# Reordering norm scalings, transposes and a routing product in the last two layers of an eight-sublayer post-norm network

## The chip, the cores and the metric

The kernel runs on one core of a Trainium2 chip. TensorE (PE) multiplies, VectorE (DVE) and ScalarE (ACT) do element work and read PSUM, GpSimd (POOL) does element work on SBUF, SyncE (SP) issues the DMAs. The metric is the device time of one execution in microseconds.

## The reference

Four layers, each an attention-like block and an FFN, and behind each of the eight blocks a residual sum and a layer norm. The input is 2 items of 1024 rows of 1024 channels in float32. The change touches the end of it, layer 2's FFN and layer 3:

```python
x = _layernorm(x + _L2_attn_ref(...))          # selective scan
x = _layernorm(x + _L2_ffn_ref(...))           # int4 weights, x @ w.T + bias
x = _layernorm(x + _L3_attn_ref(...))          # one head of 256, softmax(q k) v Wo + bo
x = _layernorm(x + _L3_ffn_ref(...))
# _L3_ffn_ref
base_out = jnp.einsum('btd,od->bto', x, base_W) + base_b
probs = jax.nn.softmax(logits, axis=-1)        # 15 routes
topk_p, topk_i = jax.lax.top_k(probs, E)       # E = 8
w = jnp.einsum('btk,btke->bte', topk_p, onehot)
h = jnp.einsum('btd,erd->bter', x, A)          # 8 experts of rank 16
lora = jnp.einsum('bter,eor->bto', h * w[..., None], B) * SCALING
return base_out + lora
```

## The kernel before

The two items run one after the other, each through all layers. An item's rows lie in SBUF as `x`, 8 row tiles of 128 rows by 1024 channels, and once more transposed as `xT` (channels on the partitions), which the products read. PSUM is one pool of 8 banks of 128x512 (`ps`, line 70); a new tile takes the bank that has been free longest.

`late` (line 1526) does layer 2's FFN and layer 3 of one item. Its order is written out by hand (`manual_schedule`, line 1745): each engine works off its instructions in program order, and TensorE waits wherever an operand or a bank is not ready. What one row tile `tt` goes through:

- `add_x` (L152): VectorE adds a PSUM tile of a product to half a row tile.
- `stats`: `ln_stats` (bn_stats L163, L164) and `ln_roots`: one small operation of VectorE (L171), Ln and Exp of ScalarE (L177, L178), and four more small ones of VectorE (L180 to L183). L180, L181 and L183 are TENSOR_TENSOR with two inputs in SBUF.
- `ln_scale` (L186): VectorE subtracts the mean and multiplies by the root, in place, one TENSOR_SCALAR over 128x1024.
- `turn_x`: `to_xT` (L124) has TensorE transpose the row tile in 8 pieces (L130) into two PSUM tiles, which VectorE (L97) and ScalarE (L99) copy to `xT`; then GpSimd adds the bias of the next product to the row tile (L1565), in place, once the transposes have read it.

The stages of `late`, in order:

1. `out_proj` (L1567) ends layer 2's attention for rows 512 to 1023 and puts tiles 0 to 3 through norm and `turn_x`. Tiles 4 to 7 get their statistics and roots.
2. int4 FFN, the loop at L1751: step n does the two halves `ffn2(wt, n, 0)` and `ffn2(wt, n, 1)` of row tile n, 8 product calls each (L104). A product call of float32 shows as two matmul records. Behind the first half come `turn_x(n - 1)`, whose norm is of this FFN, and in steps 1 to 3 the scaling and `turn_x` of tiles 4, 5, and 6 with 7, which still lack it.
3. `heads` and `values`: q, k and v.
4. Attention, the loop at L1777: for each query tile `scores` (two PSUM tiles), `exps` (maxima by VectorE, L1635; Exp by ScalarE, L1642), `turn` (8 transposes of the probabilities, L1656, copied by VectorE and ScalarE). From n = 6 on, `join(n - 6)` multiplies the mixed values by Wo, and VectorE adds the result to `x` (L1680), with `stats`. In steps 7 and 8 `turn_x(n - 7)` stands ahead of `join`.
5. `mix(1)`, `turn_x(3)`, `route(0)` (routing logits by `thin`, L112; ScalarE copies them, L1688; transposes L1691; softmax on VectorE), `rank` of four tiles (VectorE), `join` of tiles 4 to 7.
6. `experts(wa, 0)` (L1717): the routes' weights are transposed (L1722) and copied by VectorE to `prT` (L1723); the product with A goes through ScalarE into `hT` (L1726, times 2); a product of `prT` with the one-hot map `oh` spreads the routes over the experts (L1728), and VectorE multiplies `hT` by it (L1729).
7. Base FFN, the loop at L1803: `ffn3(wt, n, 0)` and `ffn3(wt, n, 1)`, 8 calls of the base weights and a ninth of `hT` with B each. `done(n - 1)` scales and stores the tile before. In steps 0 and 1 two tiles each (4, 5 and 6, 7) get `ln_scale` and `turn_x` between the halves. `route(1)`, `rank` and `experts(wa, 1)` for the upper rows are spread over steps 1 to 3.

The weights come by SP into a pool of 8 tiles, each load waiting for the last product that read the tile before; the last two weights of stage 7 are loaded when the last `join` has been done. Rows of biases have a pool of two; a load of a new row waits for the last GpSimd addition of the row it replaces.

Of the kernel before, what the change touches and what calls it, by code (L numbers as in the profile page):

```python
# [12 lines left out]
ALU = mybir.AluOpType  # L13
# [4 lines left out]
P = 128  # L18
# [4 lines left out]
KD = D // P  # L23
# [4 lines left out]
class Net:  # L28
# [1497 lines left out]
    def late(self, b, yd):  # L1526
        nc, i = self.nc, self.i
        NCH, NR = 16, 15
        rows = {"l2_fb": self.row("l2_fb"), "l3_bo": self.row("l3_bo")}
        with self.tc.tile_pool(name=self.nm("l3a"), bufs=1) as lp, self.tc.tile_pool(name=self.nm("l3p"), bufs=2) as tp:  # L1530
# [14 lines left out]
            oh = lp.tile([NR, P], F, name=self.nm("oh"))  # L1545
# [8 lines left out]
            prT = lp.tile([NR, S], F, name=self.nm("prT"))  # L1554
            hT = lp.tile([P, S], F, name=self.nm("hT"))
            wb = self.param(lp, "l3_B", [P, D])
# [5 lines left out]
            def turn_x(tt, row):  # L1562

                self.to_xT(tt)
                nc.gpsimd.tensor_tensor(self.x[:, tt, :], self.x[:, tt, :], row, ALU.add)  # L1565

            def out_proj():  # L1567

                for nh in range(2):
                    acc = [self.ps() for _ in range(4)]  # L1570
                    for c2 in range(NCH // 2):
                        w = self.w(i["l2_out"][nh, c2])
                        y = self.w()
                        for cc in range(2):
                            nc.sync.dma_start(y[:, cc * HALF : (cc + 1) * HALF], yd[2 * c2 + cc][:])
                        for cc in range(2):
                            c = 2 * c2 + cc
                            for tt in range(4):
                                nc.tensor.matmul(  # L1579
                                    acc[tt],  # L1580
                                    y[:, cc * HALF + tt * P : cc * HALF + (tt + 1) * P],
                                    w[:, cc * HALF : (cc + 1) * HALF],
                                    start=c == 0,
                                    stop=c == NCH - 1,
                                )
                        if nh == 0 and c2 == 0:
                            for tt in range(4):
                                self.ln_stats(tt)
                            self.ln_roots(list(range(4)))
                        if nh == 0 and c2 % 2 == 1:  # L1590
                            self.ln_scale(c2 // 2)
                            turn_x(c2 // 2, rows["l2_fb"])
                    for tt in range(4):
                        self.add_x(4 + tt, nh, acc[tt])

            def ffn2(wt, tt, nh):
                p = self.ps()
                self.mm(p, [(self.xcols(k, tt * P, P), wt[k][:, nh * HALF : (nh + 1) * HALF]) for k in range(KD)])
                self.add_x(tt, nh, p)
# [49 lines left out]
            def turn(tt):  # L1649
                th, q = tt // 4, tt % 4  # L1650
                pr, sm = prs.pop(tt)
                for g in range(2):
                    p = self.ps()
                    for j in range(4):
                        kt = 4 * g + j
                        nc.tensor.transpose(p[:, j * P : (j + 1) * P], pr[:, kt * P : (kt + 1) * P], self.ident)  # L1656
                    self.evac(
                        pts[th][:, 4 * g : 4 * g + 4, q * P : (q + 1) * P], p.rearrange("p (k t) -> p k t", k=4)
                    )
                r = rinv[th][:, q : q + 1]  # L1660
                nc.vector.tensor_tensor(r, sm[:, 0:1], sm[:, 1:2], ALU.add)
                nc.vector.reciprocal(r, r)
# [54 lines left out]
            def experts(wa, th):  # L1717

                ts = slice(th * HALF, (th + 1) * HALF)
                p = self.ps()  # L1720
                for j in range(4):
                    nc.tensor.transpose(p[:NR, j * P : (j + 1) * P], st[th][:, j, :], self.ident)  # L1722
                nc.vector.tensor_copy(prT[:, ts], p[:NR, :])  # L1723
                p = self.ps()
                self.mm(p, [(wa[:, k * P : (k + 1) * P], self.xcols(k, th * HALF, HALF)) for k in range(KD)])
                nc.scalar.mul(hT[:, ts], p, 2.0)  # L1726
                p = self.ps()
                nc.tensor.matmul(p, oh, prT[:, ts], start=True, stop=True)  # L1728
                nc.vector.tensor_tensor(hT[:, ts], hT[:, ts], p, ALU.mult)  # L1729

            def ffn3(wt, tt, nh):
                ns = slice(nh * HALF, (nh + 1) * HALF)
                p = self.ps()
                self.mm(
                    p,
                    [(self.xcols(k, tt * P, P), wt[k][:, ns]) for k in range(KD)]
                    + [(hT[:, tt * P : (tt + 1) * P], wb[:, ns])],
                )
                self.add_x(tt, nh, p)

            def done(tt):
# [3 lines left out]
            with self.tc.manual_schedule():  # L1745
                out_proj()
                for tt in range(4, 8):
                    self.ln_stats(tt)
                self.ln_roots(list(range(4, 8)))
                wt = [self.w(self.wq[k * P : (k + 1) * P, :]) for k in range(KD)]  # L1750
                for n in range(NT):  # L1751
                    if n >= 1:
                        self.ln_scale(n - 1)
                    ffn2(wt, n, 0)
                    if n >= 1:
                        turn_x(n - 1, rows["l3_bo"])
                    for tt in ((), (4,), (5,), (6, 7), (), (), (), ())[n]:
                        self.ln_scale(tt)
                        turn_x(tt, rows["l2_fb"])
                    ffn2(wt, n, 1)  # L1760
                    stats(n)
                self.ln_scale(7)
                wt = [self.w(i["l3_wqkv"][k]) for k in range(KD)]
                heads(wt, 0)
                turn_x(7, rows["l3_bo"])
                for tt in range(4):
                    values(wt, tt)
                heads(wt, 1)
                for tt in range(4, 8):
                    values(wt, tt)  # L1770
                row = self.row("l3_fb")
                wo = [self.w(i["l3_wo"][k]) for k in range(2)]
                wa = lp.tile([P, D], F, name=self.nm("wa"))
                nc.sync.dma_start(wa, i["l3_A"])
                wt = [self.w(i["l3_fw"][k]) for k in range(6)]
                scores(0)
                for n in range(1, NT + 1):  # L1777
                    exps(n - 1)
                    if n >= 7:
                        self.ln_scale(n - 7)  # L1780
                    if n < NT:
                        scores(n)
                    if n == 5:
                        mix(0)
                    if n >= 7:
                        turn_x(n - 7, row)
                    if n >= 6:
                        join(wo, n - 6)
                    turn(n - 1)
                self.ln_scale(2)  # L1790
                join(wo, 3)
                turn_x(2, row)
                self.ln_scale(3)
                mix(1)
                turn_x(3, row)
                route(0)
                for n in range(4):
                    rank(0, n)
                for n in range(4):
                    join(wo, 4 + n)  # L1800
                wt += [self.w(i["l3_fw"][k]) for k in range(6, KD)]
                experts(wa, 0)
                for n in range(NT):  # L1803
                    if n >= 1:
                        done(n - 1)
                    if n >= 2:
                        self.load_x(b + 1, n - 2)
                    ffn3(wt, n, 0)
                    if n < 2:
                        for tt in (4 + 2 * n, 5 + 2 * n):  # L1810
                            self.ln_scale(tt)
                            turn_x(tt, row)
                    if n == 1:
                        route(1)
                    if n == 3:
                        experts(wa, 1)
                    ffn3(wt, n, 1)
                    stats(n)
                    if n == 1 or n == 2:
                        rank(1, 2 * n - 2)  # L1820
                        rank(1, 2 * n - 1)
                self.load_x(b + 1, NT - 2)
                done(NT - 1)
                self.load_x(b + 1, NT - 1)
# [119 lines left out]
```

## Time and profile before

| | |
|---|---|
| runs | 5371.23, 5376.52, 5391.84 us; median 5376.52 |
| profiled execution | 5374.18 us, its span 5372.4 us |
| TensorE clock granted, mean | 0.964 |
| TensorE waiting, 2195 to 2705 us (item 0) | 31.4 us in 11 waits at L130, 7.1 in one at L1728, 1.4 at L1691, 0.3 at L112 |

Stages of item 0 (us from the span's start; item 1 is the same some 2659 us later). The columns are the time that TensorE, VectorE and GpSimd were busy, and the TensorE clock granted, as a share of full speed.

| stretch | PE | DVE | POOL | PEclk |
|---|---|---|---|---|
| 2195 to 2337, end of `out_proj`, int4 FFN | 129.62 of 142 | 57.31 | 25.77 | 0.95 |
| 2337 to 2421, q, k, v | 84.00 of 84 | 7.36 | 2.35 | 1.00 |
| 2421 to 2500, attention and joins | 69.31 of 79 | 35.81 | 4.68 | 0.94 |
| 2500 to 2532, mix, routing, joins | 30.95 of 32 | 17.66 | 4.71 | 1.00 |
| 2532 to 2596, experts, base FFN steps 0 and 1 | 46.92 of 64 | 27.33 | 9.37 | 0.81 |
| 2596 to 2705, rest of the base FFN | 109.00 of 109 | 36.70 | 0.00 | 1.00 |

In a row of a timeline stand the start, the duration, engine, line and operation, output and input with shapes, and in brackets how long the engine had been idle and what released it. A row with x8 merges eight instructions.

### The profile page before, as it was taken

To read this page: it belongs to the slowest core of one execution; us is meant where nothing else is said; L and a number is where in the kernel's file an instruction comes from. 1 tells how busy PE (TensorE), PEld (TensorE's weight loads), DVE (VectorE), ACT (ScalarE), POOL (GpSimd) and SP (SyncE) were. 2 spreads that over 40 slices of the span, in tenths; PEclk is the share of its full clock that TensorE was granted. 3 is DMA by queue.
4 is the path that set the end of the run, shared out by engine and by line. 5 is a ranking of instruction groups with operands and counts; after the bars stand their busy time and mean duration, and the time that the engine had idled before them with its cause. 6 is when DMAs were issued, how large, how long until landed. Compare 5 with 4: busy or idle time off the path is not lost.

```text
span 5372.4 us, 51914 instructions
## 1 busy us (share of the span) xinstructions
PE 4953.8 (92%) x17608; PEld 2461.5 (46%) x17608; DVE 3202.9 (60%) x4386; ACT 1944.0 (36%) x3935; POOL 2023.6 (38%) x1195
## 2 busy tenths in 40 slices
PE   8879988999999999998998899789999999999988
PEld 3346745444444444454433476454444444444533
DVE  5453256279999997314364422551899999953243
ACT  2421232367756552001024211323677665410110
POOL 1013110077778884100010220200877888821010
PEclk9999989999999999999999999899999999999989
DMA  2145311277787996101121432113877889950100
GB/s 92 40 149 180 100 50 50 97 225 210 209 243 213 262 265 196 63 32 43 47 72 40 145 121 90 53 53 104 243 206 214 244 225 262 262 170 32 63 8 32
DMA packets 263356, 726.00 MB, mean 135 GB/s; under 512 B 37040, under 2 KB 54576, under 8 KB 263092
## 3 DMA queue, kind: packets, MB, share of 16 engines
q1 hardware_dynamic: 256820, 701.70, 43.5%
q0 software_dynamic: 6272, 20.98, 1.1%
q8 instruction: 141, 2.31, 0.2%
q14 instruction: 123, 1.01, 0.1%
HBM read 617.43 MB, written 103.02 MB: 134 GB/s over the span
## 4 chain that ended last, share of the span: by engine, by line
PE 68%; DVE 13%; ACT 4%; DMA 3%; issue 2%; POOL 1%; SPq 0%; DVEq 0%; ACTq 0%; POOLq 0%
PE ps L104 26%; PE ps L1364 7%; PE ps L1254 6%; PE ps L606 5%; PE ps L1283 4%; PE ps L1579 4%; DVE h L1261 4%; PE ps L1403 3%; DVE h L1272 2%; PE ps L130 2%; PE ps L1317 2%; ACT ps L1256 1%; DVE st L163 1%; DMA h<-dxd 1%; DVE x L186 1%
## 5 line engine op out<-in xcount | busy, mean ns | idle before, releaser
L1246 POOL TENSOR_TENSOR h<-h,br 128x1024 f32<-128x1024 f32 x512 | 1204.1, 2373 | 28.6 <-DMA h<-dxd 17.9
L1256 ACT ACTIVATE ps<-ps,l_Alog 128x512 f32<-128x512 f32 x1024 | 669.0, 660 | 686.7 <-PE ps L1254 678.9
L1254 PE MATMUL ps<-hi,rep 128*128 128x512 f32 x1024 | 757.9, 740 | 23.3 <-DVE h L1261 14.9
L1261 DVE TENSOR_TENSOR_SCAN h<-ps,h 128x512 f32<-128x512 f32 x512 | 604.7, 1208 | 159.4 <-ACT ps L1256 159.4
L1261 DVE TENSOR_TENSOR_SCAN h<-ps,hst,h 128x512 f32<-128x512 f32 x512 | 632.5, 1266 | 16.0 <-ACT ps L1256 15.5
L1272 DVE TENSOR_TENSOR h<-h,ps 128x1024 f32<-128x1024 f32 x512 | 610.4, 1192 | 0.0
L104 PE MATMUL ps<-w,xT 128*128 128x512 f32 (+1 forms) x1280 | 520.8, 564 | 0.0
L1364 PE MATMUL ps<-xT,w 128*128 128x512 f32 x1024 | 516.4, 608 | 0.0
L1283 PE MATMUL ps<-h,sel 128*32 128x512 f32 x2048 | 410.1, 615 | 72.6 <-DVE h L1272 72.2
L1565 POOL TENSOR_TENSOR x<-x,row 128x1024 f32<-128x1024 f32 x48 | 112.6, 2345 | 876.7 <-PE ps L130 876.7
L152 DVE TENSOR_TENSOR x<-x,ps 128x512 f32<-128x512 f32 x192 | 128.9, 681 | 526.2 <-PE ps L104 379.2
L1254 PE MATMUL ps<-lo,rep 128*128 128x512 f32 x1024 | 408.8, 399 | 0.0
L104 PEld LDWEIGHTS ps<-w,xT 128*128 128x128 f32 x1280 | 248.0, 195 | 257.1 <-issue 250.2
L1254 PEld LDWEIGHTS ps<-hi,rep 128*128 128x128 f32 x1024 | 196.5, 192 | 350.0 <-issue 239.5
L104 PE MATMUL ps<-xT,w 128*128 128x512 f32 x768 | 336.8, 594 | 0.0
L177 ACT ACTIVATE rs<-mv 128x1 f32<-128x1 f32 (+2 forms) x88 | 17.9, 203 | 767.1 <-DVE mv L171 766.8
L130 PE MATMUL ps<-ident,x 128*128 128x128 f32 x1024 | 152.7, 301 | 148.5 <-DVE x L186 138.4
L1254 PEld LDWEIGHTS ps<-lo,rep 128*128 128x128 f32 x1024 | 196.3, 192 | 200.1 <-issue 195.3
L1212 POOL TENSOR_TENSOR e<-e,one 128x512 f32<-128x512 f32 x64 | 81.6, 1274 | 547.7 <-ACT one L1209 375.8
L1364 PEld LDWEIGHTS ps<-xT,w 128*128 128x128 f32 x1024 | 189.2, 192 | 175.3 <-issue 149.9
L1403 PE MATMUL ps<-w,w 128*128 128x512 f32 x512 | 268.0, 605 | 0.0
L1317 PE MATMUL ps<-xT,w 128*128 128x512 f32 x512 | 266.1, 605 | 2.0 <-DVE h L1261 1.9
(283 smaller groups left out, 7402.2 us busy)
## 6 DMA issues: line engine op xcount, KB each, us to landing
h<-dxd SPq DMA_DIRECT2D x512, 512.0 KB, 6.4
w<-l_in SPq DMA_DIRECT2D x128, 512.0 KB, 5.8
w<-l_out SPq DMA_DIRECT2D x96, 512.0 KB, 5.9
w<-l_conv SPq DMA_DIRECT2D x54, 512.0 KB, 3.5
w<-cvd SPq DMA_DIRECT2D x36, 512.0 KB, 3.2
w<-l_fw SPq DMA_DIRECT2D x32, 512.0 KB, 5.7
xcd<-xo SPq DMA_DIRECT2D x64, 256.0 KB, 2.1
szd<-zo SPq DMA_DIRECT2D x64, 256.0 KB, 3.7
```

The lines of the kernel that those rows point to most:

```text
L104: self.nc.tensor.matmul(out, lhsT, rhs, start=j == 0, stop=j == n - 1)
L130: nc.tensor.transpose(p[:, j * P : (j + 1) * P], self.x[:, tt, k * P : (k + 1) * P], self.ident)
L606: nc.tensor.matmul(w["p", j // 2][:, 256 * (j % 2) : 256 * (j % 2) + 256], w["w"][j][:, k * P : (k + 1) * P], moving(th, j, k), start=k == ...
L1246: nc.gpsimd.tensor_tensor(hs[k], hs[k], norms[of(k)[0]][1].unsqueeze(1).to_broadcast([P, 2, HALF]), ALU.mult)
L1254: nc.tensor.matmul(dA[k, m], rep[:, 8 * jj + 4 * m + q, :], hl[u, c][n], start=n == 0, stop=n == 1)
L1256: nc.scalar.activation(dA[k, m], dA[k, m], AF.Exp, scale=A[:, g : g + 1])
L1261: nc.vector.tensor_tensor_scan(hs[k][:, m, :], dA.pop((k, m)), hs[k][:, m, :], hst[:, g : g + 1] if u else 0.0, ALU.mult, ALU.add)
L1272: nc.vector.tensor_tensor(hs[k], hs[k], norms[of(k)[0]][3].unsqueeze(1).to_broadcast([P, 2, HALF]), ALU.mult)
L1283: nc.tensor.matmul(py[u, c][32 * j : 32 * j + 32, :], self.sel[:, q, :], hs[k - 1 + j // 2][:, j % 2, :], start=False, stop=q == 3,)
L1317: nc.tensor.matmul(p, w["w"][:, k * P : (k + 1) * P], self.xcols(k, u0, HALF), start=k == 0, stop=k == KD - 1)
L1364: nc.tensor.matmul(p, w["w"][:, k * P : (k + 1) * P], self.xcols(k, u * HALF, HALF), start=k == 0, stop=k == KD - 1)
L1403: nc.tensor.matmul(p, y[:, cc, t * P : (t + 1) * P], wt[:, cc * HALF : (cc + 1) * HALF], start=c2 == 0 and cc == 0, stop=last,)
```

## The change

In the two FFN loops the scalings of tiles 4 to 7 go ahead of the first half of their step, so that in the program of VectorE they stand ahead of the add of that half, and in time ahead of GpSimd's addition that follows the first `turn_x` of the step. Their `turn_x` stays where it was. In the attention loop `turn_x` of steps 7 and 8 goes behind `join` and `turn`. `experts` no longer does the product with `oh` and the multiplication itself, but returns a function that does; for rows 0 to 511 `ffn3(wt, 0, 0)` calls it behind its sixth product call, with its own PSUM tile still open, and for the upper rows it is called at once, as before. The number of instructions is the same on every engine.

```diff
@@ -1724,18 +1724,22 @@
                 p = self.ps()
                 self.mm(p, [(wa[:, k * P : (k + 1) * P], self.xcols(k, th * HALF, HALF)) for k in range(KD)])
                 nc.scalar.mul(hT[:, ts], p, 2.0)
-                p = self.ps()
-                nc.tensor.matmul(p, oh, prT[:, ts], start=True, stop=True)
-                nc.vector.tensor_tensor(hT[:, ts], hT[:, ts], p, ALU.mult)
-
-            def ffn3(wt, tt, nh):
+
+                def weigh():
+                    p = self.ps()
+                    nc.tensor.matmul(p, oh, prT[:, ts], start=True, stop=True)
+                    nc.vector.tensor_tensor(hT[:, ts], hT[:, ts], p, ALU.mult)
+
+                return weigh
+
+            def ffn3(wt, tt, nh, weigh=None):
                 ns = slice(nh * HALF, (nh + 1) * HALF)
                 p = self.ps()
-                self.mm(
-                    p,
-                    [(self.xcols(k, tt * P, P), wt[k][:, ns]) for k in range(KD)]
-                    + [(hT[:, tt * P : (tt + 1) * P], wb[:, ns])],
-                )
+                for k in range(KD):
+                    nc.tensor.matmul(p, self.xcols(k, tt * P, P), wt[k][:, ns], start=k == 0, stop=False)
+                    if weigh and k == 5:
+                        weigh()
+                nc.tensor.matmul(p, hT[:, tt * P : (tt + 1) * P], wb[:, ns], start=False, stop=True)
                 self.add_x(tt, nh, p)
 
             def done(tt):
@@ -1749,13 +1753,14 @@
                 self.ln_roots(list(range(4, 8)))
                 wt = [self.w(self.wq[k * P : (k + 1) * P, :]) for k in range(KD)]
                 for n in range(NT):
-                    if n >= 1:
-                        self.ln_scale(n - 1)
+                    late = ((), (4,), (5,), (6, 7), (), (), (), ())[n]
+
+                    for tt in ([n - 1] if n else []) + list(late):
+                        self.ln_scale(tt)
                     ffn2(wt, n, 0)
                     if n >= 1:
                         turn_x(n - 1, rows["l3_bo"])
-                    for tt in ((), (4,), (5,), (6, 7), (), (), (), ())[n]:
-                        self.ln_scale(tt)
+                    for tt in late:
                         turn_x(tt, rows["l2_fb"])
                     ffn2(wt, n, 1)
                     stats(n)
@@ -1782,11 +1787,11 @@
                         scores(n)
                     if n == 5:
                         mix(0)
-                    if n >= 7:
-                        turn_x(n - 7, row)
                     if n >= 6:
                         join(wo, n - 6)
                     turn(n - 1)
+                    if n >= 7:
+                        turn_x(n - 7, row)
                 self.ln_scale(2)
                 join(wo, 3)
                 turn_x(2, row)
@@ -1799,21 +1804,22 @@
                 for n in range(4):
                     join(wo, 4 + n)
                 wt += [self.w(i["l3_fw"][k]) for k in range(6, KD)]
-                experts(wa, 0)
+                weigh = experts(wa, 0)
                 for n in range(NT):
                     if n >= 1:
                         done(n - 1)
                     if n >= 2:
                         self.load_x(b + 1, n - 2)
-                    ffn3(wt, n, 0)
-                    if n < 2:
-                        for tt in (4 + 2 * n, 5 + 2 * n):
-                            self.ln_scale(tt)
-                            turn_x(tt, row)
+                    late = (4 + 2 * n, 5 + 2 * n) if n < 2 else ()
+                    for tt in late:
+                        self.ln_scale(tt)
+                    ffn3(wt, n, 0, weigh if n == 0 else None)
+                    for tt in late:
+                        turn_x(tt, row)
                     if n == 1:
                         route(1)
                     if n == 3:
-                        experts(wa, 1)
+                        experts(wa, 1)()
                     ffn3(wt, n, 1)
                     stats(n)
                     if n == 1 or n == 2:
```

## The prediction

> **What bounds the kernel now.** I read the page first (busy shares, then the chain that ended last), then the waits of TensorE in the two stretches where the changed code runs, then the timelines of TensorE, VectorE and GpSimd there.
>
> ```profile
> PE 4953.8 (92%) x17608; PEld 2461.5 (46%) x17608; DVE 3202.9 (60%) x4386; ACT 1944.0 (36%) x3935; POOL 2023.6 (38%) x1195
> PE 68%; DVE 13%; ACT 4%; DMA 3%; issue 2%; POOL 1%; SPq 0%; DVEq 0%; ACTq 0%; POOLq 0%
> ```
>
> TensorE is the bound: busy 92% of the span, 68% of the chain. The changed code runs twice, once per batch item, at 2195 to 2705 us and 4853 to 5372 us. TensorE's waits of the first stretch:
>
> ```profile
> PE ps L130 <- DVE x L186: 31.4, 11, 6.1
> PE ps L1728 <- DVE prT L1723: 7.1, 1, 7.1
> ```
>
> The second stretch answers with the same two lines. So 38.5 us of idle TensorE per item, nearly all of what it waits for there, hang on VectorE's norm scaling (L186) and on one copy (L1723), both touched by the change. The first such wait, in the timelines of TensorE, VectorE and GpSimd:
>
> ```profile
> 2220.40 1.04 PE L130 MATMUL ps<-ident,x 128*128 128x128 f32 x8
> 2224.46 1.09 PE L130 MATMUL ps<-ident,x 128*128 128x128 f32 x8 [3.03 <-DVE x L186]
> 2225.39 15.60 PE L104 MATMUL ps<-w,xT 128*128 128x512 f32 x32
> 2301.52 13.90 PE L104 MATMUL ps<-w,xT 128*128 128x512 f32 x32
> 2217.32 0.81 DVE L186 TENSOR_SCALAR x<-x,mv,rs 128x1024 f32<-128x1024 f32 x1
> 2221.88 2.53 DVE L186 TENSOR_SCALAR x<-x,mv,rs 128x1024 f32<-128x1024 f32 x1
> 2221.52 2.34 POOL L1565 TENSOR_TENSOR x<-x,row 128x1024 f32<-128x1024 f32 x1 [74.05 <-PE ps L130]
> ```
>
> The reader should see three things. The scaling takes 0.81 us alone and 2.53 us when it meets GpSimd's bias: the bias ends at 2223.86, the scaling 0.55 us later, so it was held until then. TensorE stands 3.03 us for it. And the 32 products behind the wait take 15.60 us instead of 13.90: the clock granted is lower after the wait (0.81 over 2532 to 2596 us, 1.00 over 2337 to 2421). A wait costs its idle time and some 1.7 us more.
>
> **The Trainium skill's rule on that.** "TensorE: Matmul & The Clock Gate", section "HAM oscillation — how this bites in real kernels", puts the limit at idle gaps of about 3.4 us. By the rule the 3.0 and 3.1 us waits would cost no clock, and the first stage below would gain its idle time alone, 12.4 us per item. By the row it gains 18.3. I take the row: in this trace a half-speed stretch follows waits of 2.55, 3.03 and 3.12 us, and none follows 1.06 us.
>
> **The parts, per item.** Durations are of item 0; one product call is two records of 0.43 us, so 8 calls take 6.87; a turn of one row tile (8 transposes) takes 0.87.
>
> *A, int4 FFN: `ln_scale` of tiles 4 to 7 moved ahead of `ffn2(wt, n, 0)`.* The same scalings, 0.73 us each back to back. The normal step is 14.61 us (2286.04 to 2300.65). Steps 1 to 3 run from 2220.40 to 2286.04, 65.64 us, for three normal steps and four extra turns, 43.83 + 3.48 = 47.31. Loss 18.33 (item 1: 65.83, 18.5). After: the scaling of tile n-1 starts about 3.6 us after the step's last add; one more makes +0.73, in step 3 two more, +1.5. In step 3 that is 2258.24 + 2.3 = 2260.5, against transposes at 2261.31. The cover is the 6.87 us of `ffn2(wt, n, 0)`; without it the up to 1.5 us would show. GpSimd's biases of the step before ended 5 to 7 us earlier, so these scalings cost 0.73, not 2.53. Biases now run in pairs (4.7 us), in step 3 in three (7.0); their readers are adds of later steps. The row-bias load on SP behind GpSimd moves along. Gain 18.3, bounds 15 and 18.5.
>
> *B, attention joins: `turn_x(n-7)` behind `join` and `turn`.* Nothing is added; on TensorE `turn_x(0)` goes behind `join(1)` and `turn(6)`, `turn_x(1)` behind `join(2)` and `turn(7)`. Before:
>
> ```profile
> 2474.09 1.50 PE L130 MATMUL ps<-ident,x 128*128 128x128 f32 x8 [2.55 <-DVE x L186]
> 2487.25 1.94 PE L130 MATMUL ps<-ident,x 128*128 128x128 f32 x8 [6.08 <-DVE x L186]
> 2499.30 1.07 PE L130 MATMUL ps<-ident,x 128*128 128x128 f32 x8 [1.06 <-DVE x L186]
> ```
>
> From the end of `scores(7)` (2471.37) to `turn_x(2)` (2499.30) 27.93 us pass for 13.8 us of work (three joins of 3.44, four turns). After: `join(1)` 2471.37 to 2474.80 (its PSUM banks are those that `join(0)`'s adds freed at 2468), `turn(6)` to 2475.67, `turn_x(0)` to 2476.54, `join(2)` to 2479.97. Then `turn(7)` waits for `exps(7)`, queued on VectorE behind join 1's adds, statistics, root and copies. This chain hung on `join(1)`'s second add, which moves from 2480.34 to 2475.01; its first reduction moves from 2484.74 to 2479.4, plus 0.6 for the xT copy that now stands ahead. There is a further delay. The bias of tile 0 now runs at about 2476.6 to 2479.0, and the root's first TENSOR_TENSOR, with two SBUF inputs, falls due at 2477.9. What such an op does beside GpSimd:
>
> ```profile
> 1523.70 0.17 DVE L180 TENSOR_TENSOR rsq<-rr 128x12 f32<-128x12 f32 x1 [0.52 <-ACT rr L178]
> 1523.91 2.25 DVE L181 TENSOR_TENSOR rsq<-rsq,ss 128x12 f32<-128x12 f32 x1
> 1526.40 2.32 DVE L183 TENSOR_TENSOR rr<-rr,rsq 128x12 f32<-128x12 f32 x1
> 1523.78 2.35 POOL L1246 TENSOR_TENSOR h<-h,br 128x1024 f32<-128x1024 f32 x1 [2.00 <-DMA h<-dxd]
> ```
>
> L181 is held until the GpSimd op is over. So +1.1, the reductions start at 2481.2, and 2.5 us later (two reductions, two small ops, the first Exp) `turn(7)` can start: 2483.7, a new wait of 3.7 us with a spell of slow clock. On VectorE the scaling of tile 2 ends at 2491 to 2491.7, TensorE is ready at 2489.2 (full clock) to 2492: `turn_x(2)` at 2491.7. Gain 7.6. Without the hold 9.4; with two slow spells and the hold met twice 4; with no wait at all 14.1.
>
> *C, experts: the product of routes with `oh` inside `ffn3(wt, 0, 0)`, behind its sixth product.* Before, TensorE stops 7.08 us at L1728 for the copy of the routes (VectorE at 2546.00, behind ranks, adds and statistics of four tiles), and the slow clock follows: from 2539.65 to the end of the FFN's first half at 2558.73, 19.08 us. After: six calls, 5.16, to 2544.81; the wait shrinks to 1.92 (the copy still lands at 2546.73); routes' product 0.86; two calls 1.72; last product 0.86: end at 2550.17. The multiplication of hT now stands behind two scalings, which end at 2548.2, and itself ends by 2548.9, ahead of its reader at 2549.3. Weights 6 and 7 are issued by 2532.7 with 7.3 us to land, needed at 2547.6. Gain 8.5. A wait of 1.92 lies between the 1.06 that cost no clock and the 2.55 that did; 0 to 1.7, nearer the first: 0.1. Take 8.4.
>
> *D, base FFN: scalings of tiles 4 to 7 ahead of `ffn3(wt, n, 0)`.* As in A. Step 0: 2558.73 to 2575.99, 17.26, becomes two turns and 7.72: 9.46, gain 7.8. Step 1: 2575.99 to the routing transposes at 2595.41, 19.42, becomes 7.72 + 1.74 + 2.63 (as at 2515.32 to 2517.95) and about 0.6, since the routing product waits for the last copies of two turns in a row: 12.69, gain 6.7. Bounds 12 and 15.
>
> The sum: 18.3 + 7.6 + 8.4 + 7.8 + 6.7 = 48.8 per item, 97.6 in all. Everything else keeps its order on every queue and hangs on TensorE's progress, so it moves along. The profiled execution took 5374.18 us (span 5372.4), 2.3 below the median 5376.52. 5374.2 − 97.6 = 5276.6; with most of that 2.3 back, 5278.
>
> **Rivals.**
>
> *The wait moves (B and C give little).* For it: `turn(7)` then waits for VectorE, and the routes' copy is no earlier. If B returns nothing and C half, the gain is 18.3 + 4.2 + 14.5 = 37 per item: 5300. Against it: the second add's place in B's chain.
>
> *The scaling was not the cause.* A wait is put to what ended last; another releaser would leave 5374. Against it: 0.81 against 2.53 beside the bias, in both items.
>
> *Slower: GpSimd's biases in a row hold VectorE's root.* Place: the two-input ops of `ln_roots` (L180, L181, L183) in some 14 FFN steps per item. Price: up to three holds of 2.3, 7 us, less VectorE's 2.5 us of slack, 4.5 per step: 2 × 14 × 4.5 = 126 against the 98 gained: 5402. It decides once biases still run when the root falls due, about 10 us after a step's last turn. The longest row, three, ends after 7.0; so it should not happen outside B.
>
> **How the numbers follow.** All as worked out: 0.80, 5278, by itself 5262 to 5295. The wait moves: 0.12, 5300. Not the cause: 0.04, 5374. Slower: 0.04, 5402. The lower end has B nearly without a wait and C without slow clock (5262); the upper end takes in the second case. A measurement of this kernel can tell about 0.5%, 27 us, from no change. Faster by more 0.92, same 0.05, slower 0.03 (the slower rival may stop short of that).
>
> **What would show it.** In the profile after: in the FFN stages no wait of L130 on L186 is left and every L186 there takes about 0.81; after 32 products at 13.90 throughout; in the joins one wait of 3 to 4 us at L1656 for the Exp and one L180 stretched to about 1.2; one wait of about 1.9 us for the copy of the routes, six products earlier. I am wrong if L130 still waits in A or D, or if L1656 waits over 6 us.

## The result and the profile after

| | before | after |
|---|---|---|
| median, measured side by side | 5373.88 us (4 runs) | 5284.69 us (4 runs) |
| ratio, 95% interval | | 0.9832 [0.9805, 0.9858] |
| profiled execution (span) | 5374.18 (5372.4) us | 5284.6 (5282.9) us |
| TensorE busy; idle in the span | 4953.8; 418.6 us | 4924.3; 358.6 us |
| mean granted clock | 0.964 | 0.970 |

The kernel is 89.2 us faster; 97.6 were forecast, and 5278 us (5262 to 5295) for the median. The interval of the ratio stands for a gain of 76 to 105 us, so the medians alone do not show that the gain fell short of the forecast. Of the 89.5 us that the span lost, 60.0 are idle time of TensorE and 29.5 are busy time: the same 17608 matmuls ran at a higher clock. The page of the changed kernel, busy times and the chain:

```profile
PE 4924.3 (93%) x17608; PEld 2453.8 (46%) x17608; DVE 3184.5 (60%) x4386; ACT 1943.2 (37%) x3935; POOL 2022.9 (38%) x1195
PE 69%; DVE 13%; ACT 4%; DMA 2%; issue 2%; POOL 1%; SPq 0%; DVEq 0%; ACTq 0%; POOLq 0%
```

The bound is the same. A row of the next view names the reader, its releaser, and the waiting time in us: total, times, longest. TensorE's waits of the changed kernel in item 0's stretch, 2195 to 2660 us:

```profile
PE ps L1656 <- ACT pr L1642: 3.5, 1, 3.5
PE ps L1730 <- DVE prT L1723: 1.9, 1, 1.9
...
PE ps L130 <- DVE x L186: 1.1, 1, 1.1
```

Where 31.4 us in 11 waits on the scaling and 7.1 for the routes stood, 1.1 and 1.9 are left, and one new wait of 3.5 for the Exp. Item 1 differs only in L130: 1.8.

**The int4 FFN**, timelines of TensorE, VectorE and GpSimd:

```profile
2220.54 1.91 PE L130 MATMUL ps<-ident,x 128*128 128x128 f32 x16
2222.29 13.90 PE L104 MATMUL ps<-w,xT 128*128 128x512 f32 x32
2251.51 2.78 PE L130 MATMUL ps<-ident,x 128*128 128x128 f32 x24
2254.13 13.90 PE L104 MATMUL ps<-w,xT 128*128 128x512 f32 x32
...
2248.43 2.26 DVE L186 TENSOR_SCALAR x<-x,mv,rs 128x1024 f32<-128x1024 f32 x3
...
2252.62 6.97 POOL L1565 TENSOR_TENSOR x<-x,row 128x1024 f32<-128x1024 f32 x3 [10.82 <-PE ps L130]
```

No turn has a bracket, so none waits: two and three tiles are turned in a row (x16, x24). The three scalings together take 2.26 us, where one had taken 2.53, because GpSimd's three biases now start 1.9 us after the last of them. The 32 products behind take 13.90, not 15.60.

**The joins**, the same three timelines:

```profile
2465.11 1.47 PE L1656 MATMUL ps<-ident,pr 128*128 128x128 f32 x8 [3.48 <-ACT pr L1642]
2473.53 1.10 PE L130 MATMUL ps<-ident,x 128*128 128x128 f32 x8 [1.11 <-DVE x L186]
...
2459.36 1.27 DVE L180 TENSOR_TENSOR rsq<-rs 128x1 f32<-128x1 f32 x1 [0.50 <-ACT rs L178]
2468.41 2.31 DVE L180 TENSOR_TENSOR rsq<-rs 128x1 f32<-128x1 f32 x1 [0.50 <-ACT rs L178]
...
2458.28 2.34 POOL L1565 TENSOR_TENSOR x<-x,row 128x1024 f32<-128x1024 f32 x1 [107.89 <-PE ps L130]
2468.36 2.34 POOL L1565 TENSOR_TENSOR x<-x,row 128x1024 f32<-128x1024 f32 x1 [7.75 <-PE ps L130]
```

L180 works on 128 numbers and takes 0.16 us undisturbed. Here it ends at 2460.63 and 2470.72, when the bias beside it ends (2460.62 and 2470.70). The first hold delays the Exp for which L1656 waits, the second the scaling for which L130 waits.

**The experts' stretch**, TensorE's timeline in item 0 and in item 1:

```profile
2521.01 1.12 PE L1730 MATMUL ps<-prT,oh 15*128 15x512 f32 x2 [1.94 <-DVE prT L1723]
2522.06 1.99 PE L1739 MATMUL ps<-w,xT 128*128 128x512 f32 x4
...
2524.74 1.91 PE L130 MATMUL ps<-ident,x 128*128 128x128 f32 x16
...
2541.94 1.91 PE L130 MATMUL ps<-ident,x 128*128 128x128 f32 x16
...
5137.29 1.12 PE L1730 MATMUL ps<-prT,oh 15*128 15x512 f32 x2 [1.95 <-DVE prT L1723]
5138.34 3.37 PE L1739 MATMUL ps<-w,xT 128*128 128x512 f32 x4
```

The same wait stands in both items, and after it the same four records take 1.99 us in one and 3.37 in the other. The turns of the two base FFN steps behind it (2524.74 and 2541.94) wait for nothing.

**Stage by stage.** Times are in us. A: start of the first turn of step 1 to that of step 4. B: end of `scores(7)` to `turn_x(2)`. C: end of the product with A to the end of the base FFN's first half. D: from there to the routing transposes. Records of TensorE overlap by some 0.16 us, so an end here is where the next record could start; C's forecast is 19.23 less the 8.4 that were worked out.

| stretch | before, items 0 and 1 | after | forecast | gain, both items |
|---|---|---|---|---|
| A | 65.64, 65.83 | 47.32, 47.32 | 47.31 | 36.8 |
| B | 27.93, 28.12 | 20.68, 19.72 | 20.3 | 15.7 |
| C | 19.23, 19.3 | 10.98, 12.68 | 10.8 | 14.9 |
| D | 36.68, 36.8 | 22.09, 22.09 | 22.15 | 29.3 |

Together 96.7 us, of 97.6 forecast. Yet the span lost only 89.5. The missing 7 us lie in stretches that the change does not touch, 5.4 of them in 1800 matmuls of item 1's layers 0 and 1. That stretch before, then after; the columns are length, busy time of TensorE, its weight load, VectorE, ScalarE and GpSimd, granted clock and DMA:

```profile
2703.20:3127.90 424.70, 377.16 (x1802) 186.48 (x1801) 205.67 (x370) 128.23 (x246) 77.08 (x94) 0.96 0.26 89
```

```profile
2654.60:3084.70 430.10, 383.82 (x1802) 191.93 (x1801) 205.86 (x370) 128.14 (x246) 76.97 (x94) 0.93 0.26 88
```

TensorE was busy 6.7 us longer over the same 1802 records, at a clock of 0.93 instead of 0.96; VectorE, ScalarE and GpSimd did theirs in equal times. The waits of the stretch also match (22.3 before and 22.4 after at L130, all others within 1.5 us). In this stretch it is clock, not a new wait.

### The profile page after: what moved, and what is told of

Same layout as the page of the kernel before. It is cut to its first block, busy times and chain, and to the rows that moved or that the text cites. A ratio compares the mean times of both kernels' runs of the same rounds, so it can differ in the third digit from the quotient of the medians.

```text
span 5282.9 us, 51916 instructions
## 1 busy us (share of the span) xinstructions
PE 4924.3 (93%) x17608; PEld 2453.8 (46%) x17608; DVE 3184.5 (60%) x4386; ACT 1943.2 (37%) x3935; POOL 2022.9 (38%) x1195
## 3 DMA queue, kind: packets, MB, share of 16 engines
q8 instruction: 141, 2.31, 0.2%
## 4 chain that ended last, share of the span: by engine, by line
PE 69%; DVE 13%; ACT 4%; DMA 2%; issue 2%; POOL 1%; SPq 0%; DVEq 0%; ACTq 0%; POOLq 0%
PE ps L104 21%; PE ps L1364 7%; PE ps L1254 6%; PE ps L606 5%; DVE h L1261 5%; PE ps L1283 5%; PE ps L1579 4%; PE ps L1739 4%; PE ps L1403 3%; DVE h L1272 2%; PE ps L1317 2%; PE ps L130 2%; ACT ps L1256 1%; DVE st L163 1%; PE ps L327 1%
## 5 line engine op out<-in xcount | busy, mean ns | idle before, releaser
L104 PE MATMUL ps<-w,xT 128*128 128x512 f32 (+1 forms) x768 | 278.3, 521 | 0.0
L1115 DVE SCALAR_TENSOR_TENSOR ps<-xp,l_convw,ps 128x512 f32<-128x512 f32 x192 | 144.5, 753 | 186.3 <-ACT ps L1110 181.7
L763 POOL TENSOR_TENSOR s<-s,l1r 128x512 f32<-128x512 f32 x64 | 66.4, 1039 | 450.0 <-DVE l1r L762 444.1
```

What stands on the lines that cost most here:

```text
L104: self.nc.tensor.matmul(out, lhsT, rhs, start=j == 0, stop=j == n - 1)
```

## The experiments

Each of the first four makes one part of the change alone, on the kernel before. Lines left out of an edit are marked by three dots.

**A alone** (a_only), the scalings of the int4 FFN:

```diff
-                    if n >= 1:
-                        self.ln_scale(n - 1)
+                    late = ((), (4,), (5,), (6, 7), (), (), (), ())[n]
+
+                    for tt in ([n - 1] if n else []) + list(late):
+                        self.ln_scale(tt)
                     ffn2(wt, n, 0)
                     if n >= 1:
                         turn_x(n - 1, rows["l3_bo"])
-                    for tt in ((), (4,), (5,), (6, 7), (), (), (), ())[n]:
-                        self.ln_scale(tt)
+                    for tt in late:
                         turn_x(tt, rows["l2_fb"])
```

> The kernel before with part A alone (scalings ahead of the first half in the int4 FFN; nothing left out). Theory: the four waits per item behind a scaling held by GpSimd's bias vanish with their slow clock; steps 1 to 3 take 47.3 us instead of 65.6, every scaling there 0.73 to 0.81 us; the whole is 36.6 us faster, ratio 0.993. Rival one, the clock rule of 3.4 us: only the idle time comes back, 24.8 us, ratio 0.995, and products behind the former waits stay at 15.6. Rival two, the scaling was not the cause: ratio 1.000.

Measured 5337.35 us, 0.9931 [0.9904, 0.9958]. A takes 47.32 us in both items, and L130's waits fall to 19.0 in 7. The products behind the former waits take 13.90 us, so rival one, 24.8 us with products still at 15.6, is refuted by the stretch; the interval of the median, 23 to 52 us, would not part the two.

**B alone** (b_only), the order of the joins:

```diff
-                    if n >= 7:
-                        turn_x(n - 7, row)
                     if n >= 6:
                         join(wo, n - 6)
                     turn(n - 1)
+                    if n >= 7:
+                        turn_x(n - 7, row)
```

> The kernel before with part B alone (transposes behind join and turn; nothing left out). Theory: from the end of the last scores to the transposes of tile 2 some 20.2 us instead of 27.9, with one wait of 3.5 us at the transposes of the probabilities and one L180 stretched to about 1.2 us by GpSimd's bias; 15 us faster in all, ratio 0.997. Rival, the bias doesn't matter there: wait of 2.4 us, 18.8 us faster. Rival, the wait only moves: ratio 1.000.

Measured 5358.74 us, 0.9975 [0.9967, 0.9983]. B takes 20.61 and 19.71 us. The wait at L1656 is there, 3.5 us, without any other part: it belongs to this order.

**C alone** (c_only), the product with `oh`:

```diff
...
+                for k in range(KD):
+                    nc.tensor.matmul(p, self.xcols(k, tt * P, P), wt[k][:, ns], start=k == 0, stop=False)
+                    if weigh and k == 5:
+                        weigh()
...
```

> The kernel before with part C alone (the routes' product inside the first half of the base FFN; nothing left out). Theory: the wait for the copy of the routes is 1.9 us instead of 7.1, and from the end of the product with A to the end of the FFN's first half 11.0 us pass instead of 19.2, up to 1.7 more where the wait falls into one clock window; 13 to 16.5 us faster in all, ratio 0.997. Rival, the multiplication or the last two weights come late and the ninth product waits instead: a wait before L1742 and less than half of that.

Measured 5356.76 us, 0.9965 [0.9952, 0.9978]. The routes' wait is 1.9; C takes 10.98 us in both items. TensorE's timeline of D in this kernel, where D is still the old one, shows the two sizes of wait beside each other:

```profile
2547.92 1.09 PE L130 MATMUL ps<-ident,x 128*128 128x128 f32 x8 [1.57 <-DVE x L186]
2552.04 1.56 PE L130 MATMUL ps<-ident,x 128*128 128x128 f32 x8 [3.03 <-DVE x L186]
2553.39 8.30 PE L1739 MATMUL ps<-w,xT 128*128 128x512 f32 x16
```

The scaling that meets no bias costs 1.57, the one behind a bias 3.03, and the 16 records after it 8.30 instead of 7.03.

**D alone** (d_only), the scalings of the base FFN:

```diff
+                    late = (4 + 2 * n, 5 + 2 * n) if n < 2 else ()
+                    for tt in late:
+                        self.ln_scale(tt)
                     ffn3(wt, n, 0)
-                    if n < 2:
-                        for tt in (4 + 2 * n, 5 + 2 * n):
-                            self.ln_scale(tt)
-                            turn_x(tt, row)
+                    for tt in late:
+                        turn_x(tt, row)
```

> The kernel before with part D alone (scalings ahead of the first half in steps 0 and 1 of the base FFN; nothing left out). Theory: step 0 from the end of its first half to the end of the second 9.5 us instead of 17.3 (more while the slow clock behind the long wait for the routes, which is still there, lasts), step 1 to the routing transposes 12.6 instead of 19.4; 27 to 29 us faster in all, ratio 0.995. If the four parts are independent, their gains sum to that of the whole change, some 97 us in the changed stretches. Rival, they overlap (one part's gain is the other's clock): the sum of the four is over 105 or under 85.

Measured 5351.36 us, 0.9957 [0.9944, 0.997]. Its steps take 9.48 and 12.61 us, as in the whole change: 29 us off D in both items together, but 22.1 in the median. In its profile the same 1800 matmuls of item 1's layers 0 and 1 take 435.4 us, against 424.7 in the kernel before.

The four gains, 36.1, 14.7, 16.7 and 22.1, sum to 89.7 us; the whole change gave 89.2. From the four intervals the sum is known to about 18 us. The stretches say it more sharply: A, B and D take the same time alone as together, and so does C where its wait cost no clock, so no part takes from another.

**Is it the bias beside the scaling, or the scaling's place?** bias_behind leaves every scaling where the kernel before has it, and queues GpSimd's biases of a step behind the step's last transposes:

```diff
                     if n >= 1:
-                        turn_x(n - 1, rows["l3_bo"])
-                    for tt in ((), (4,), (5,), (6, 7), (), (), (), ())[n]:
+                        self.to_xT(n - 1)
+                    late = ((), (4,), (5,), (6, 7), (), (), (), ())[n]
+                    for tt in late:
                         self.ln_scale(tt)
-                        turn_x(tt, rows["l2_fb"])
+                        self.to_xT(tt)
+                    for tt in reversed(late):
+                        bias(tt, rows["l2_fb"])
+                    if n >= 1:
+                        bias(n - 1, rows["l3_bo"])
```

(in the base FFN's loop likewise).

> The kernel before, its scalings left where they were, but in both FFN loops GpSimd's biases of a step are queued in reverse order, so that none starts before the step's last transposes (nothing left out). It parts the hold by GpSimd from the order on VectorE. Theory, the hold is the larger half: every L186 there takes 0.81 us, the waits of L130 shrink from 3.0 to 3.1 us to 1.3 to 1.6, and single waits of that size leave the clock full: int4 FFN steps 1 to 3 take 53 us instead of 65.6, the base FFN's two steps 3.5 to 8 us less per item; 32 to 42 us faster in all, ratio 0.993. Rival, the order alone sets the wait and GpSimd is a bystander: waits of 3 us stay, ratio 1.000.

Measured 5341.62 us, 0.9941 [0.9924, 0.9957] against 5376.46. All its scalings of item 0 take 0.80 to 0.82 us (a row of the `x` tile's view: shortest, median and longest in ns). Below it TensorE's timeline, item 0 and then item 1:

```profile
L186 DVE TENSOR_SCALAR x<-x,mv,rs x25: 796/807/815, 2213.5 to 2638.1; 128x1024 f32<-128x1024 f32 x25
...
2253.03 1.06 PE L130 MATMUL ps<-ident,x 128*128 128x128 f32 x8 [1.39 <-DVE x L186]
2255.25 1.07 PE L130 MATMUL ps<-ident,x 128*128 128x128 f32 x8 [1.16 <-DVE x L186]
2256.15 13.90 PE L104 MATMUL ps<-w,xT 128*128 128x512 f32 x32
...
4894.19 1.06 PE L130 MATMUL ps<-ident,x 128*128 128x128 f32 x8 [1.39 <-DVE x L186]
4896.41 1.94 PE L130 MATMUL ps<-ident,x 128*128 128x128 f32 x8 [1.16 <-DVE x L186]
4898.14 14.54 PE L104 MATMUL ps<-w,xT 128*128 128x512 f32 x32
```

A takes 53.36 us in item 0: of the 18.3 lost, 12.3 were the meeting with GpSimd and its clock, 6.0 the place of the scaling. That refutes the rival "the scaling was not the cause". Item 1 takes 54.83 with the same waits: the clock again. So the split is good to some 1.5 us.

**Are the joins held by the biases?** free_roots is the changed kernel with the biases of tiles 0 and 1 queued behind tile 2's:

```diff
                     if n >= 7:
-                        turn_x(n - 7, row)
+                        self.to_xT(n - 7)
...
                 turn_x(2, row)
+                bias(0, row)
+                bias(1, row)
```

> The changed kernel with GpSimd's biases of tiles 0 and 1 queued behind that of tile 2 (nothing left out). Theory: the L180 of the root of tile 1 is no longer held (0.16 us), the wait for the Exp at the transposes of the probabilities shrinks from 3.5 to 2.4 us, and the stretch from the last scores to the transposes of tile 2 takes 18.0 to 19.0 us instead of 19.7 to 20.7; 2 to 5 us faster than the changed kernel. Rival, the hold costs nothing since the chain is late anyway: wait still 3.5 us, no gain.

Measured 5279.54 us, 0.9827 [0.981, 0.9843]. VectorE's and GpSimd's timelines, and TensorE's wait for the Exp:

```profile
2463.09 0.16 DVE L180 TENSOR_TENSOR rsq<-rs 128x1 f32<-128x1 f32 x1 [0.50 <-ACT rs L178]
2469.64 2.25 DVE L181 TENSOR_TENSOR rsq<-rsq,mv 128x1 f32<-128x1 f32 x1
...
2467.23 6.95 POOL L1568 TENSOR_TENSOR x<-x,row 128x1024 f32<-128x1024 f32 x3 [121.05 <-PE ps L130]
...
PE ps L1659 <- ACT pr L1645: 2.4, 1, 2.4
```

The L180s of tiles 1 and 2 take 0.16 us again, and the wait for the Exp is 2.4 us instead of 3.5. L130 waits 0.6 us in item 0 and not at all in item 1; B takes 17.42 and 18.09 us. So these two holds cost 1.6 to 3.3 us per item. The row of three biases now holds the root of tile 3 (L181 2.25 us, L183 2.08), for which no turn waits. The total does not show it: in this profile C took 14.1 us in both items, 3.1 more than its best, as the routes' wait was followed by a longer slow spell.

**The routes' product two calls later**: weigh_behind_eighth has `k == 7` instead of `k == 5`.

> The changed kernel with the routes' product behind the eighth product call instead of the sixth (nothing left out). Theory: the wait for the copy of the routes shrinks from 1.9 to 0.2 to 0.4 us, and a new wait of about 1 us for the multiplication stands ahead of the ninth product; the end of the first half comes 0.9 us earlier where the clock was full and 2.5 us where it was slow, so 2 to 3.5 us in all. Rival, the multiplication behind two scalings sets the end: no gain or a loss of up to 2 us.

Measured 5282.78 us, 0.9822 [0.9806, 0.9839]. The waits of this kernel in item 0:

```profile
PE ps L1742 <- DVE hT L1731: 0.9, 1, 0.9
...
PE ps L1730 <- DVE prT L1723: 0.2, 1, 0.2
```

The medians (5282.78 and 5284.69, measured apart) do not tell the two kernels apart, but the stretch does. One wait of 1.9 has become two of 0.2 and 0.9. From the end of the product with A to the second routing logits it takes 29.7 us, in both items, and again in both items of joins_ahead_eighth below. With the product behind the sixth call, in eight item stretches of four kernels (the changed kernel twice, free_roots, joins_ahead), it took 30.4 twice, 32.1 three times and 33.8 three times: the waits were 1.93 to 1.95 us each time, the clocks unequal.

**Joins without a wait**: joins_ahead multiplies joins 2 and 3 ahead of the last turn, puts their statistics and scalings beside `mix(1)`, and `turn_x(2)`, `turn_x(3)` behind it. `product` does the two halves of a join and hands back the two additions of VectorE:

```diff
...
-                    if n >= 6:
+                    if n >= 6 and n < NT:
                         join(wo, n - 6)
+                    if n == NT:
+                        for add in [*product(wo, 2), *product(wo, 3)]:
+                            add()
                     turn(n - 1)
                     if n >= 7:
-                        turn_x(n - 7, row)
-                self.ln_scale(2)
-                join(wo, 3)
-                turn_x(2, row)
-                self.ln_scale(3)
+                        self.to_xT(n - 7)
+                bias(1, row)
+                bias(0, row)
+                for tt in (2, 3):
+                    stats(tt)
+                    self.ln_scale(tt)
                 mix(1)
-                turn_x(3, row)
+                for tt in (2, 3):
+                    turn_x(tt, row)
```

> The changed kernel with the products of joins 2 and 3 both ahead of the last transposes of the probabilities, their statistics and scalings beside the product that mixes the values, and the transposes of tiles 2 and 3 behind it (nothing left out). Theory: the waits of 3.5 us and 1.1 to 1.8 us that part B left find cover; from the last scores to the routing product 31 us instead of 36.7; 9 to 12 us faster than the changed kernel, some 0.982 minus 0.002 of the kernel before. Rival, the wait moves once more, to the mixing product, which needs the last copies of the probabilities: under 4 us gained.

Measured 5275.84 us, 0.982 [0.9804, 0.9837]. TensorE's timeline:

```profile
2462.41 1.04 PE L1659 MATMUL ps<-ident,pr 128*128 128x128 f32 x8
2463.28 1.04 PE L130 MATMUL ps<-ident,x 128*128 128x128 f32 x8
2464.64 14.00 PE L104 MATMUL ps<-pt,v 128*128 128x512 f32 x32 [0.33 <-DVE pt L97]
2478.48 1.91 PE L130 MATMUL ps<-ident,x 128*128 128x128 f32 x16
```

Of 4.6 us of waits 0.3 are left. From the end of `scores(7)` to the first routing logits it takes 30.48 us in both items; the changed kernel took 36.74 and 35.77, the kernel before 43.95 and 44.14. The stretch is as forecast (31), but the ratios of the two kernels, 0.982 and 0.9832, have overlapping intervals.

**The changed kernel once more, and the best version.** Measured side by side with a kernel before of 5366.29 us: the changed kernel (after_again), and joins_ahead with `k == 7` (joins_ahead_eighth).

> The changed kernel once more, so that the two versions below stand beside it in the same call. All theories expect its ratio to the kernel before within its interval of the first measurement, 0.981 to 0.986. Theory (clock windows in unchanged work): in its profile the stretches A, B, C, D of both items come out as before, A 47.3, B 19.7 to 20.7, C 11.0 or 12.7, D 9.5 and 12.6 us, while the time from the routing transposes of item 0 to the end of layer 2's attention of item 1, which the change leaves alone, differs from the 2269.9 us of the first profile by up to 10 us either way. Rival (the change itself costs some 7 us there): it is 2269 to 2271 again, against 2262.6 in the kernel before.

> The kernel with the products of joins 2 and 3 ahead of the last turn, and besides it the product of routes with oh behind the eighth product of the base FFN's first half instead of the sixth. Theory (what is left of the waits adds up: one wait at the probabilities' transposes, one for the routes' copy): 4 to 5 us per item less than the changed kernel in the joins, 0 to 2 in the experts' stretch (C 10.4 to 11.0 in both items), so 8 to 13 us less than the changed kernel in this call, some 0.2%. Rival (off the path or lost again to clock in unchanged work): within 4 us of it.

after_again: 5278.2 us, 0.9841 [0.9818, 0.9863]. A is 47.32 again and C takes 12.7 in both items this time. From item 0's routing transposes to the end of item 1's layer 2 attention it took 2263.4 us; the first profile of the same program took 2269.9, the kernel before 2262.6. The rival, which put 7 us there for good, had said 2269 to 2271. joins_ahead_eighth: 5268.58 us, 0.9822 [0.9805, 0.9839], 9.6 us below the changed kernel beside it, as forecast (8 to 13), though the intervals overlap.

## Why the prediction was right, and where it fell short

*What bounds it.* Right. The parts named were where the time came from, and they add (89.7 against 89.2).

*A and D, the held scaling.* Right to 0.1 us in what was to be left: 47.32 for 47.31, 9.48 for 9.46, 12.61 for 12.69. The cover named, `ffn2(wt, n, 0)`, held: 2.26 us of scalings end 0.8 us before the transposes. What the kernel before lost there was read from one profile, and that one lay high. In the eight item stretches of before, b_only, c_only and d_only, which all have the old A, it took 63.8 to 67.1 us, 65.05 on average, against 65.64 and 65.83; the old D of before, a_only and b_only took 0.4 us less on average than in before. That is some 1.1 us per item, 2.2 in all, by which the forecast gain was too large.

*The clock rule.* The prediction set aside the limit of about 3.4 us of idle time that it cites from the Trainium skill ("TensorE: Matmul & The Clock Gate", section "HAM oscillation — how this bites in real kernels") for the row with 2.55 to 3.12, and A gained 18.3 rather than 12.4. That choice is confirmed. The clock of 0.81 that the prediction read beside it is the mean of another stretch. The 1.7 us behind such a wait are one slow window, here in the kernel before around the wait of 3.03 us (length, TensorE's busy time first; the clock is the third column from the end):

```profile
2222.04:2225.45 3.41, 0.99 (x9) 0.99 (x10) 2.66 (x2) 0.02 (x1) 1.82 (x1) 1.00 0.00 0
2225.45:2228.86 3.41, 3.41 (x6) 1.35 (x6) 0.40 (x1) 0.59 (x1) 2.34 (x1) 0.50 0.02 5
2228.86:2232.28 3.42, 3.42 (x10) 1.51 (x9) 0.00 (x0) 0.00 (x0) 0.00 (x0) 1.00 0.00 0
```

A window of 3.41 us at half speed does the work of 1.7. The prediction's wording, a wait costs 1.7 us more, was too simple, see C.

*B, the joins.* Right: 20.68 and 19.72 us for 20.3. The wait was 3.48 for 3.7, and L180 was stretched to 1.27 for 1.2. Unforeseen in the main case was the second hold (L180 at 2.31); it ended in a wait of 1.1 to 1.8 at `turn_x(2)`, inside the spread given for that turn. The rival "the wait moves" was right that one appears, wrong on its size.

*C, the step that was mis-sized.* The wait came out as forecast, 1.94 for 1.92. The term "0 to 1.7, nearer the first: 0.1" for the clock behind it did not: over the eight stretches above and the two of c_only (C took 10.98 us) it cost nothing four times, 1.7 us three times and 3.3 three times. That is 1.5 on average, so some 3 us for two items.

Why an equal wait costs unequal time is to be seen in three windows of 3.41 us around it, in item 0 and then in item 1 of the changed kernel (columns as above):

```profile
2513.92:2517.33 3.41, 3.41 (x9) 1.50 (x9) 2.73 (x9) 0.41 (x2) 0.00 (x0) 1.00 0.00 0
2517.33:2520.74 3.41, 1.74 (x5) 0.43 (x3) 2.73 (x10) 0.89 (x3) 0.00 (x0) 1.00 0.01 2
2520.74:2524.16 3.42, 3.15 (x7) 1.35 (x8) 2.26 (x4) 0.00 (x0) 0.00 (x0) 1.00 0.02 5
...
5131.92:5135.33 3.41, 3.41 (x8) 1.16 (x7) 3.27 (x9) 0.00 (x0) 0.00 (x0) 1.00 0.00 0
5135.33:5138.74 3.41, 1.46 (x4) 0.59 (x4) 2.80 (x9) 0.89 (x3) 0.00 (x0) 1.00 0.00 0
5138.74:5142.16 3.42, 3.42 (x5) 1.35 (x4) 0.53 (x1) 0.00 (x0) 0.00 (x0) 0.51 0.00 0
```

In item 0 the wait fell across the edge of two windows (busy 1.74 and 3.15 of 3.41 us); in item 1 most of it fell into one (1.46), and the next window ran at half speed. Over the twelve traces, of full-speed windows busy for 0.40 to 0.45 of their length, as that of item 1, 73 of 113 were followed by a half-speed one; of those busy for 0.50 to 0.55, as that of item 0, 25 of 188. The Trainium skill, "TensorE: Matmul & The Clock Gate", section "What's actually happening", says the activity window is 3413 ns long and free-running; the traces agree: every clock record of a run starts a whole number of 3.413 us after its first, and where this grid lies to the program's start differs from run to run. So what a wait of this size costs depends on where the grid lies, as a likelihood and not as a sharp rule. One stretch does not fit neatly: in after_again's item 0 the window with the wait was busy for 0.64 of its length and was still followed by half speed.

*"Everything else keeps its order and moves along."* In order and waits it did. In clock it did not: the layers that nothing touched ran 7 us longer in this profile. Over the twelve profiles of this study the same 1800 matmuls take 424.6 to 438.0 us, 429.9 on average, with the kernel before at 424.7; for one program they took 430.1 once and 427.7 once. free_roots, which has the whole change, took 424.6, as little as the kernel before. Take all of TensorE's time that lies outside both items' stretches from the start of A to the end of D. It is 4608.3 us in before, 4616.1 and 4607.2 in the two profiles of the changed kernel, and 4607 to 4624 over all twelve; the mean is 4613.5 over the six profiles with the whole change and 4614.9 over the six others. So no lasting cost of the change shows there, and the 7 us of the first profile look like luck of the clock. Both comparisons had the changed kernel 88 to 89 us below the one before, 9 less than forecast. C's 3 us and the 2.2 of A and D leave some 4, well inside the intervals of both (76 to 105 and 74 to 98 us). Whether they are more than noise is left open.

*The slower rival.* Biases in a row did not hold a root in the FFN stages: three of them end at 2259.59 in step 3, and the root that follows (L180 at 2264.01, 0.16 us) ends ahead of the scaling at 2264.79, which takes 0.81. The one place of the changed stretches where biases hold a root is the joins, as the prediction had it.

## What to carry to other kernels

Look at the duration of a small operation, not only at its wait: a scaling of 2.53 us among ones of 0.81 names the neighbour that holds it, and queueing that neighbour later or the scaling earlier returns both the hold and the clock behind it. Where a few microseconds count, waits of TensorE of 2 us are worth splitting too: one of 1.9 cost nothing, 1.7 or 3.3 us more by chance, while waits of 0.2 and 0.9 us in its place cost no clock in four stretches. A forecast from one profile carries the clock of that profile, in the stretches that are changed and in those that are not; one unchanged stretch of some 430 us alone was 13 us wide here.

## What the runs showed of the hardware

- A VectorE operation on 128 numbers (L180, 0.16 us) that meets GpSimd's 2.34 us addition stays until that is over, to 0.02 us (1.27 and 2.31 us). The 0.81 us scaling is held likewise: 2.53 us, ending 0.55 us behind the addition.
- In the trace of before, cut into a 3.41 us grid and set beside the clock records, all 57 full-speed windows in which TensorE was busy under 0.40 were followed by a half-speed one; of 44 between 0.40 and 0.60 nine were; of those above 0.60 three in 1355. No half-speed window busy under 0.85 was followed by full speed. Over all twelve traces the first three counts are 557 of 557, 140 of 528 and 41 of 16337, and of 380 half-speed windows busy under 0.85 nine were followed by full speed.
- Two waits of 1.39 and 1.16 us, 2.2 us apart, lowered the clock in one item and not in the other: neither is long, but together they fill most of one window (busy 0.37) or fall into two (0.59 and 0.66).
